# The loads of x for layer norm 1 are begun by GpSimd in place of ScalarE

## The chip, the cores and the metric

The kernel runs on one core of a Trainium2 chip. Its time is the device time of one execution in microseconds; the figure compared is the median of several runs. One execution was also taken by the hardware profiler, and all rows shown come from that one.

## The reference, cut to what matters

The input x has 4 images of 16 x 16 positions with 1024 channels, that is 1024 tokens. Layer 0 is a lambda layer between a group norm and a residual sum; layer 1 is causal attention over the 256 tokens of an image, and then a mixture of 8 experts.

```python
# layer 0
x = x + _L0_conv_ref(_gn(x), Wq, Wk, Wv, ..., rel_pos_emb)
#   inside: Lc = softmax(k) v^T;  Yc = q Lc           (content)
#           Lp = rel_pos_emb gathered, times v;  Yp = q Lp   (position)
#           Y = Yc + Yp
# layer 1
t = _to_tokens(x)
t = t + _L1_attn_ref(_ln_t(t), W_attn, b_attn, W_proj, b_proj)
t = t + _L1_ffn_ref(_ln_t(t), gate_w, gate_b, expert_w, expert_b)
x = _from_tokens(t, x)
```

All of it is float32. The place of this change is the residual sum of layer 0, x + Y, and the first layer norm of layer 1 behind it.

## The kernel before

The 1024 tokens are 8 tiles of 128 tokens; tile t = 2 * b + nt is half nt of image b. Channels are 8 blocks of 128. Large products are done by Strassen's scheme with 7 products of half blocks in place of 8.

Layer 0 starts from the transposed input in the buffer `xn` (8 blocks of 128 channels by 1024 tokens, 4 MB), which group norm overwrites. Products of it give q (line 311 and 392), the keys (line 423) and the values `v_T` (`v_product`, line 530, in seven products whose last is number 4). VectorE puts the products together (lines 535 to 554), and ScalarE scales the four quarters of `v_T` (line 557, four instructions).

The position part is built as products of windows of the embedding with q (line 502; the windows are copied by GpSimd, some by VectorE, line 499) into `two_T`, and from there 88 transfers of SP move rows of it into their places in the buffer `s0` (`move`, line 479, 16 to 64 KB each, one after the other in SP's queue). The moves that stand last are for the lower half of the positions (ni < 8), which only the last four tiles read.

Then line 572 begins the eight loads of the untransposed x, 512 KB each, into `x_at`. This buffer has the same home as `xn` (pool `x_pool`, one buffer), so it is free when the last v product has read `xn`. The loads go in the order in which the tiles are worked: nt = 1 of the four images, then nt = 0.

For each tile, `spread` (line 583) adds the content part to `s0` (products `pc`, line 444, added by VectorE at line 452), one tile ahead, multiplies `s0` by `v_T` (products `py`, line 595), and VectorE adds the result to x in `x_at` (line 602). `layer_norm` (line 184) follows on VectorE (statistics at line 189) and ScalarE (line 162). For six of the eight tiles the normalised rows are then turned into columns by way of DRAM: SP copies them out (line 204) and reads them back in quarters (line 174, four transfers a tile), and VectorE transposes those (line 179, two tiles later). GpSimd meanwhile adds the projection bias to x and writes it to `x_rows` in DRAM (lines 629 and 630). The buffers of the quarters are the spent buffers `emb` and `s_w`. Afterwards come the value products of the attention (line 656) with the weights `w_v`, loaded at line 121 by SP.

Each engine runs its instructions in the order of its queue. From line 613 on the order is the order of the program (`manual_schedule`); before that a scheduler of the framework orders the instructions of each engine, and the eight loads and the four scalings of v_T belong to this part. A transfer reports by a semaphore. The framework deals out eight of them in turn to the transfers that SP and ScalarE begin, in the order of the program, and eight others to those of GpSimd; before a transfer is begun, the former transfer on its semaphore must have landed. In the program before, ScalarE's queue holds three scalings of v_T, the first load of x, the fourth scaling, and the other seven loads. The first load waits for the end of the last v product and for the move that used its semaphore before it (the eighth from the last). The load of w_v (line 121) follows the last move in SP's queue, and the first copy of line 204 has the same semaphore as this load.

Of the kernel before, what the change touches and what calls it, by code (L numbers as in the profile page):

```python
# [39 lines left out]
P = 128  # L40
# [29 lines left out]
def kernel(  # L70
# [27 lines left out]
    nc = tc.nc  # L98
# [120 lines left out]
    with ExitStack() as layer0:  # L219
# [347 lines left out]
        xs = [x_at[:, t, :] for t in range(NT)]  # L567
        late = pool(x_home, "late", 2, side="right")
        tiles = [(b, nt) for nt in (1, 0) for b in range(B)]
        for b, nt in tiles:  # L570
            t = 2 * b + nt
            nc.scalar.dma_start(xs[t], x[ts(t, P), :])

# [7 lines left out]
        def spread(i):  # L583
            b, nt = tiles[i]
            t = 2 * b + nt
            if i == 0:
                content(b, nt)
            if i + 1 < NT:
                content(*tiles[i + 1])
            for hp in range(2):  # L590
                py = mm(f"py{t}_{hp}")
                for hl in range(2):
                    bh = b * HEADS0 + 2 * hp + hl
                    for mh in range(2):
                        nc.tensor.matmul(  # L595
                            py[:, ts(hl, M)],
                            s0[:, mh, ts(nt, S2), :, bh].rearrange("p i j -> p (i j)"),
                            v_T[:, mh, ts(b, M)],
                            start=(mh == 0),
                            stop=(mh == 1),  # L600
                        )
                nc.vector.tensor_add(xs[t][:, ts(hp, HALF)], xs[t][:, ts(hp, HALF)], py)
            return t
# [11 lines left out]
        for i in range(NT - 1):  # L615
            t = spread(i)
# [16 lines left out]
        t = spread(NT - 1)  # L633
# [4 lines left out]
    with ExitStack() as attention:  # L638
# [299 lines left out]
        with tc.manual_schedule():  # L938
            for i in range(written, len(steps) + lag):
                if i == written:  # L940
                    w_p.append(w_tile("w_p0", W_projT[:, :HALF]))
                if i == 28:
# [3 lines left out]
                    xs = [x_pool.tile([P, C], F32, tag=f"x{t}", name=f"xb{t}") for t in range(NT)]  # L946
# [5 lines left out]
                if 32 <= i < 34:  # L952
                    b, nt = tiles[NT - 34 + i]
                    t = 2 * b + nt
# [718 lines left out]
```

## Time and profile before

| | us |
|---|---|
| median of 3 runs | 1247.86 (1246.52 to 1249.15) |
| the profiled execution | 1245.87 |
| its span, first to last instruction | 1244.1 |
| TensorE busy | 1222.2 |
| VectorE busy | 741.6 |
| GpSimd busy | 404.0 |
| ScalarE busy | 220.0 |

The rows read as follows. A row of the timeline has the start and the length in us, the engine, the line of the kernel, the operation, the written and the read buffer, and the number of instructions; in brackets stands how long the engine was idle before it and what ended that. PE is TensorE, DVE VectorE, ACT ScalarE, POOL GpSimd, SP SyncE; ACTq and SPq are the queues in which ScalarE and SyncE begin transfers. A transfer's time to landing runs from its issue to the report that its data has arrived. The granted clock of TensorE is given as a share of its full speed.

### The profile page before, as it was taken

The numbers are of one execution on the slowest core, as the hardware profiler recorded it, in microseconds if no ns is written. First come the engines' busy times: TensorE is split into PE (matmuls) and PEld (weight loads), VectorE is DVE, ScalarE is ACT, GpSimd is POOL, SyncE is SP. The second block draws the span as 40 slices with busy tenths as digits, with TensorE's granted clock in tenths as the row PEclk, the third lists the DMA queues.
The fourth block names the chain that finished last, engine by engine and source line by source line (L and its number), as shares of the span: only waits on it lengthen the run. The fifth ranks groups of instructions, "written<-read, shape, count | busy, mean of one in ns | idle before, by whom it ended". The sixth has DMA issues, their size and how long they took to land.

```text
span 1244.1 us, 13324 instructions
## 1 busy us (share of the span) xinstructions
PE 1222.2 (98%) x4796; PEld 633.7 (51%) x4796; DVE 741.6 (60%) x1333; ACT 220.0 (18%) x514; POOL 404.0 (32%) x462
## 2 busy tenths in 40 slices
PE   9999998899999999999999999999999999999998
PEld 5445883678884444444444444444344434434443
DVE  5796635477432666657554867765656656565642
ACT  3310110221000222222121422110210111111110
POOL 0041340246000222222232115445452745363521
PEclk9999999899999999999999999999999999999999
DMA  9002023872202535353383657383856575656442
GB/s 349 21 1 81 5 53 72 303 251 69 68 1 68 153 106 156 105 174 108 101 286 118 196 218 254 72 236 89 240 129 173 109 229 154 156 128 190 101 82 54
DMA packets 94121, 169.77 MB, mean 136 GB/s; under 512 B 11968, under 2 KB 48848, under 8 KB 94048
## 3 DMA queue, kind: packets, MB, share of 16 engines
q1 hardware_dynamic: 75680, 112.68, 27.8%
q0 software_dynamic: 14992, 47.25, 16.2%
q10 hardware_dynamic: 3376, 8.91, 2.0%
q8 instruction: 40, 0.66, 0.2%
q14 instruction: 33, 0.27, 0.1%
HBM read 116.12 MB, written 48.50 MB: 132 GB/s over the span
## 4 chain that ended last, share of the span: by engine, by line
PE 89%; SPq 4%; DVE 3%; DMA 2%; ACT 1%; issue 1%; POOL 0%; DVEq 0%; ACTq 0%; POOLq 0%
PE p L1440 31%; PE pqk L656 16%; PE pv L656 8%; PE po L897 7%; SPq L479 4%; PE pq_pair L392 4%; PE left L1482 3%; PE pq L311 3%; PE pk L423 2%; PE sc L812 2%; PE pa L881 2%; PE rest L1496 2%; PE pT L502 1%; DMA w_v<-in_W_attnT_dram 1%; PE py L595 1%; PE last_pe L1598 1%
## 5 line engine op out<-in xcount | busy, mean ns | idle before, releaser
L1009 POOL DMA_INDIRECT w_e_xg<-rows,gather x146 | 157.0, 1075 | 57.3 <-issue 41.1
L1440 PE MATMUL p<-w_e,A 128*128 128x512 f32 x368 | 163.2, 593 | 1.3 <-DVE slot L1275 1.3
L854 POOL TENSOR_TENSOR s_q<-s_q,total 128x128 f32<-128x128 f32 (+1 forms) x128 | 66.1, 547 | 276.3 <-DVE total L851 276.3
L897 PE MATMUL po<-w_p,y_T 128*128 128x512 f32 x256 | 118.5, 604 | 0.0
L1440 PEld LDWEIGHTS p<-w_e,A 128*128 128x128 f32 x368 | 69.6, 190 | 89.9 <-issue 89.4
L1032 POOL DMA_INDIRECT out_dram<-y,add x32 | 56.5, 1767 | 178.2 <-ACT y L1446 114.8
L1440 PE MATMUL p<-T,S 128*128 128x512 f32 x256 | 112.7, 592 | 0.0
L1446 ACT ACTIVATE y<-y,slot 128x512 f32<-128x512 f32 x64 | 46.1, 721 | 335.5 <-DVE y L1454 177.4
L840 ACT ACTIVATE s_q<-s,top 128x256 f32<-128x256 f32 (+1 forms) x128 | 56.6, 443 | 186.2 <-issue 142.1
L656 PE MATMUL pqk<-ln,w_qk 128*128 128x512 f32 x192 | 85.6, 595 | 0.0
L1440 PEld LDWEIGHTS p<-T,S 128*128 128x128 f32 x256 | 48.6, 190 | 60.8 <-issue 60.5
L897 PEld LDWEIGHTS po<-w_p,y_T 128*128 128x128 f32 x256 | 45.9, 190 | 47.9 <-issue 46.9
L179 DVE STREAM_TRANSPOSE A<-w_e_xg 128x1024 f32<-128x1024 f32 x32 | 39.6, 1238 | 48.8 <-DMA w_e_xg<-rows,gather 48.7
L656 PE MATMUL pqk<-T,S_qk 128*128 128x512 f32 x128 | 58.5, 599 | 0.0
L656 PEld LDWEIGHTS pqk<-ln,w_qk 128*128 128x128 f32 x192 | 36.0, 190 | 43.4 <-issue 42.1
L1440 PE MATMUL p<-T,A 128*128 128x512 f32 x128 | 57.5, 592 | 0.0
L1440 PE MATMUL p<-w_e,S 128*128 128x512 f32 x128 | 57.5, 592 | 0.0
L311 PE MATMUL pq<-w_q,xn 128*128 128x512 f32 x96 | 44.5, 599 | 0.3 <-ACT xn L291 0.3
L656 PE MATMUL pv<-w_v,ln 128*128 128x256 f32 x192 | 43.5, 380 | 0.2 <-ACT ln L215 0.2
L1482 PE MATMUL left<-w_e,one 128*32 128x512 f32 x312 | 41.8, 593 | 0.0
L1440 PEld LDWEIGHTS p<-w_e,S 128*128 128x128 f32 x128 | 24.3, 190 | 30.6 <-issue 30.6
L1440 PEld LDWEIGHTS p<-T,A 128*128 128x128 f32 x128 | 24.3, 190 | 30.6 <-issue 30.1
(326 smaller groups left out, 1893.8 us busy)
## 6 DMA issues: line engine op xcount, KB each, us to landing
w_e<-in_expert_w_dram SPq DMA_DIRECT2D x14, 2048.0 KB, 12.2
s_rows<-s_q SPq DMA_DIRECT2D x32, 384.0 KB, 2.5
s_rows<-s_rows SPq DMA_DIRECT2D x128, 96.0 KB, 2.3
w_qk<-in_W_attnT_dram SPq DMA_DIRECT2D x8, 1024.0 KB, 5.9
xn<-in_xT_dram SPq DMA_DIRECT2D x8, 512.0 KB, 7.2
w_q<-in_Wq_dram SPq DMA_DIRECT2D x16, 256.0 KB, 7.0
x_at<-in_x_dram ACTq DMA_DIRECT2D x8, 512.0 KB, 8.9
w_v<-in_W_attnT_dram SPq DMA_DIRECT2D x2, 2048.0 KB, 11.3
```

What stands on the lines that cost most here:

```text
L311: nc.tensor.matmul(pq, xn[:, c, ts(t, P)], w_q[kc][:, c, :], start=(c == 0), stop=(c == NC - 1))
L392: nc.tensor.matmul(bank, a[:, c, :], b[:, c, :], start=(c == 0), stop=(c == NC // 2 - 1))
L479: nc.sync.dma_start(*m[2:])
L656: nc.tensor.matmul(bank, stationary(c), moving(c), start=(c == 0), stop=(c == NC // 2 - 1))
L840: nc.scalar.activation(blocks(h, qt), s[:, h, cols].rearrange("p (b f i) -> p b f i", f=Q, i=32), AF.Exp, bias=top[:, qt, h : h + 1], accu ...
L854: nc.gpsimd.tensor_mul(blocks(h, qt), blocks(h, qt), total[:, qt, h : h + 1].unsqueeze(2).unsqueeze(3).to_broadcast([P, 1 + qt, Q, 32]),)
L897: nc.tensor.matmul(po, y_T[:, c, ts(t, P)], w_p[j][:, c, :], start=(c == 0), stop=(c == NC - 1))
L1009: nc.gpsimd.indirect_dma_start(out=row[:, g, :], out_offset=None, in_=table[: (TOK - P) * Q, :] if e in SHORT else table, in_offset=bass.I ...
L1032: nc.gpsimd.indirect_dma_start(out=out[: TOK - P, :] if e in SHORT else out, out_offset=bass.IndirectOffsetOnAxis(ap=add[:slots, e, k : k ...
L1440: nc.tensor.matmul(bank, a[:, c, :], b[:, c, :], start=(c == 0), stop=(c == NC // 2 - 1))
L1446: nc.scalar.mul(y[i][:, ts(j, HALF)], y[i][:, ts(j, HALF)], slot[:, e, 1, 2 * pair + i : 2 * pair + i + 1])
L1482: nc.tensor.matmul(bank[ts(i, 32), :], stationary, w[of][j][:, c, :], start=(c == 0), stop=(c == NC - 1))
```

## The change

The loop at line 570 gives the eight loads to GpSimd's queue in place of ScalarE's. Nothing else in the program's text is changed.

```diff
         tiles = [(b, nt) for nt in (1, 0) for b in range(B)]
         for b, nt in tiles:
             t = 2 * b + nt
-            nc.scalar.dma_start(xs[t], x[ts(t, P), :])
+            nc.gpsimd.dma_start(xs[t], x[ts(t, P), :])
```

In the built program the four scalings of v_T then stand next to each other in ScalarE's queue. The eight loads stand in GpSimd's queue between its last window copy and its first addition of line 629. They take their semaphores from GpSimd's eight, so the later transfers of SP move on by eight turns, which is the same semaphore again for all but one: the load of w_v takes the semaphore that the first load of x had, and the first copy of line 204 now follows a move on its semaphore.

## The prediction

> **What bounds the kernel now.** I read three views of the page first: the busy times, the slices and the chain that ended last.
>
> ```profile
> PE 1222.2 (98%) x4796; PEld 633.7 (51%) x4796; DVE 741.6 (60%) x1333; ACT 220.0 (18%) x514; POOL 404.0 (32%) x462
> PE 89%; SPq 4%; DVE 3%; DMA 2%; ACT 1%; issue 1%; POOL 0%; DVEq 0%; ACTq 0%; POOLq 0%
> PE p L1440 31%; PE pqk L656 16%; PE pv L656 8%; PE po L897 7%; SPq L479 4%; PE pq_pair L392 4%; PE left L1482 3%; PE pq L311 3%; PE pk L423 2%; PE sc L812 2%; PE pa L881 2%; PE rest L1496 2%; PE pT L502 1%; DMA w_v<-in_W_attnT_dram 1%; PE py L595 1%; PE last_pe L1598 1%
> ```
>
> TensorE is the bound almost everywhere: it idles 22 us of 1244.1, so a change to some loads can only win where one of those few stalls lies. The pieces of the chain that are not TensorE (SP's queue at line 479, then the load of w_v) lie between 164 and 247 us, which is where the eight loads are begun (219.3 to 226.9 us). So I next read the timeline of TensorE there (start, duration, idle time before and what ended it):
>
> ```profile
> 206.43 7.03 PE L444 MATMUL pc<-q,k_q 128*128 128x512 f32 x16
> 213.30 0.59 PE L595 MATMUL py<-v_T,s 128*128 128x256 f32 x2
> 220.62 5.88 PE L595 MATMUL py<-v_T,s 128*128 128x256 f32 x14 [6.73 <-ACT v_T L557]
> 226.34 3.60 PE L444 MATMUL pc<-q,k_q 128*128 128x512 f32 x8
> 229.77 3.71 PE L595 MATMUL py<-v_T,s 128*128 128x256 f32 x16
> 249.11 3.70 PE L444 MATMUL pc<-q,k_q 128*128 128x512 f32 x8 [1.68 <-DVE s L452]
> ```
>
> Two stalls: 6.73 us that a ScalarE instruction ends, and 1.68 us that VectorE ends. After the first, 14 products take 5.88 us where 16 take 3.71 a round later. The timeline of ScalarE says what held it:
>
> ```profile
> 205.12 0.81 ACT L557 ACTIVATE v_T<-v_T,vp 128x512 f32<-128x512 f32 x1 [0.38 <-DVE v_T L552]
> 219.32 0.39 ACTq L572 DMA_DIRECT2D x_at<-in_x_dram  x1
> 219.76 0.81 ACT L557 ACTIVATE v_T<-v_T,vp 128x512 f32<-128x512 f32 x1 [13.83 <-DMA s<-two_T]
> 220.51 6.85 ACTq L572 DMA_DIRECT2D x_at<-in_x_dram  x7
> ```
>
> The fourth scaling of v_T stands in ScalarE's queue behind the first load of x, and that load waits until a move s<-two_T of SP has landed. Its own input was ready at 207.3 (line 554 on VectorE, 206.63 + 0.69). The order of the built program names the wait: SP's and ScalarE's DMAs take turns on eight completion semaphores, and the load must wait for the move that used its semaphore last, which SP issues at 217.2. Its real condition, the end of the last v product that reads the buffer, is met at 206.5. The other stall, by the timelines of SP and VectorE:
>
> ```profile
> 212.74 9.54 SPq L479 DMA_DIRECT2D s<-two_T  x15
> 222.38 0.53 SPq L121 DMA_DIRECT2D w_v<-in_W_attnT_dram  x1
> 237.06 0.35 SPq L204 DMA_DIRECT2D ln_rows<-ln_rows  x1
> 242.56 1.83 SPq L174 DMA_DIRECT2D emb<-ln_rows  x4
> ```
>
> ```profile
> 223.67 0.69 DVE L602 TENSOR_TENSOR x_at<-x_at,py 128x512 f32<-128x512 f32 x1 [9.48 <-DMA x_at<-in_x_dram]
> 247.24 1.25 DVE L179 STREAM_TRANSPOSE ln<-emb 128x1024 f32<-128x1024 f32 x1 [3.78 <-DMA emb<-ln_rows]
> ```
>
> The first layer-norm rows are ready at 230.76 (line 162), but their copy to DRAM starts at 237.06, because in the built program it has the same semaphore as w_v, which lands 14.61 us after its issue: it shares the DMA engines with the loads of x.
>
> **The change part by part.** *Removed from ScalarE:* one wait and eight issues (0.39 us median). The four scalings then follow each other, so the fourth runs at 207.4 to 208.2, and TensorE goes on at 213.30 without a gap. The 16 products of the first py take 3.55 us in later rounds (229.77 to 233.32) against 13.04 us now (213.30 to 226.34): 9.49 us less. Of this 6.73 is the idle time; 2.76 is the slower clock after it, 0.50 in the rows between 222.4 and 225 us. The table load of 1.28 us at 227.39 moves ahead too and is on no path (VectorE releases the next ScalarE step, 0.21 us).
>
> *Added to GpSimd:* eight issues, in its queue behind the window copies, which end at 183.8, and before line 629, first at 230.84. GpSimd is idle 47.01 us between. The order of the changed program gives these loads other completion semaphores, whose former users landed before 130 us, so they wait only for VectorE at 199.9, TensorE at 206.5 and an old ScalarE step. They start at about 206.6. The nearest row is line 951 (the same 512 KB from DRAM, on GpSimd): 0.55 us each and 5.0 to 9.1 us to land, so issues end at about 211.5. The first x is wanted at 215.3 (line 602 starts 1.97 us after py does, 229.77 to 231.74): 206.6 + 6.9, the median, gives 213.5; with 9.1 it is 215.7, 0.4 late, and a spare PSUM bank covers that. Later ones are wanted 7 us apart and land about 2.3 us apart. Cost: nothing, in the cover of the 16 pc products; without the cover each microsecond of a late first x is a microsecond of TensorE.
>
> The Trainium skill, "SBUF — State Buffer", section "SBUF: two separate sides", speaks against this: descriptors of GpSimd's DMAs cannot be written while VectorE runs in its two-port mode. VectorE is busy 3.44 of the 8.40 us from 206.6, with additions that read PSUM; even if each of these five blocked GpSimd for its whole 0.69 us, x would come 3.4 us later. No row here shows such a block. "DMA: Bandwidth & Descriptors", section "Issuing engines are not separate DMA queues", says another engine saves only issue time: by that alone the gain would be 8 x 0.39 = 3.1 us of ScalarE, none of it TensorE's. The 13.83 us row says that what is saved is a place in a queue.
>
> *Moved: the transfers.* The 4.19 MB of x now run beside 24 moves of SP, from 206.6 to 222.4, not beside w_v. A move lands in 2.0 us alone and 4.1 to 5.1 us beside the loads (those issued from 218.5 on). SP issues one each 0.637 us and reuses a semaphore each eighth, so 5.1 us is just what it bears without slowing. Then w_v starts at 222.4 as now.
>
> *The next thing that is late* is the first quarter chain, no longer held by w_v's semaphore (the copy of rows now follows an early move), but queued behind w_v on SP and in the transfers. With DMA engines full from 206.6 on, at the 398 GB/s of 225 to 237 us, in us of full engines: x 10.5; moves 5.6 (share 0.28 for 8.4 us, 0.44 for 7.4 us); w_v 5.3; the copied rows 1.3; the first write of x_rows 1.3. Sum 24.0; with 1.9 latency (fastest 512 KB write of GpSimd, 3.2, less 1.3) the copy lands at 232.5. (The same sum on the run of before puts w_v at 238.4; it landed at 237.0.) From landing to the transpose it took 4.75 us (242.49 to 247.24), so the transpose starts at 237.25 and the fifth round's pc 1.87 later, at 239.1 (before: 249.11). TensorE alone would be there at 213.30 + 3.55 + (249.11 - 1.68 - 226.34) = 237.94. So a stall of about 1.2 us stays.
>
> *Sum:* 249.11 - 239.1 = 10.0 us; or 9.49 + 1.68 - 1.2. Everything after is TensorE back to back, with waits relative to it, so the gain reaches the end. Bounds: w_v at the 7.9 us of the second w_v gives a transpose by about 235 and no stall, gain 11.2; w_v at 14.6 as now gives 237.0, copied rows 1.3, then 4.75 + 1.87: pc at 244.9, gain 4.2. I take the middle sum, since a bounded amount of data has to pass. The profiled execution took 1245.87 us (span 1244.1 and 1.8 around it) and would take 1235.9; the median of the runs is 1247.86, 2.0 above it, so 1237.9.
>
> **The rivals.** *The quarter chain takes the whole place of the stall.* If moves land in 7.2 us (the quarters s_rows beside GpSimd's loads at 618 to 630 us, median), SP issues one each 0.90 us, w_v starts 6.3 us later, and up to that much of the gain goes: gain 3 to 6, 1242 to 1245 us. For it: 5.1 is the edge already. Against: while moves wait, x finishes earlier, and the 7.2 us rows also queue behind a 2 MB load of SP.
>
> *Slower.* The same place, with a price: each us by which the moves end later than about 223 costs one. All the gain is gone when the transpose stands at 247.24 again, that is 10.0 us later, or 8 x (0.637 + 10.0/24) = 8.4 us to land; slower by over 2.5 us needs 9.3 us for all 24 moves. At 10 us it is 24 x 0.613 = 14.7 later and 4.7 slower: 1253. No 64 KB move in this trace comes near.
>
> *Nothing changes.* x is late after all: if the first load waits for GpSimd's descriptors or lands only at 223.7 as now, the py round drains as before and only the semaphore of w_v is gained, 0 to 1.7 us: 1246 to 1248. It would need 17 us to land, against 9.1 at most.
>
> **How the numbers follow.** Forecast (gain 6.5 to 11.2): 0.76. Chain takes most (gain 2.5 to 6.5): 0.13. Gain over 11.2, if the chain is faster and SP's later turns too: 0.03. No change: 0.04. Slower: 0.04. About 0.2%, 2.5 us, is what a measurement of this kernel can tell from no change. So faster 0.92, same 0.04, slower 0.04. The range reaches from 1247.86 - 11.2 less 0.4 for the spread of the runs, 1236.2, into the chain case at a gain of 5.4: 1242.5.
>
> **What would show it.** Right: the four scalings of v_T in a row by 208.5; TensorE without a gap at 213.3 and a granted clock of 1.0 through 225; x begun on GpSimd from 206.6, first landing before 215; w_v issued near 222.4 and landing before 233; line 204 issued within 1 us of w_v; the first transpose near 237; span near 1234. Wrong: a wait of VectorE at line 602 for x; SP's moves more than 0.7 us apart and w_v after 225; a gap of TensorE over 3 us before the fifth pc, all the more if its clock falls there again; or a new gap after 273 us that takes the gain back.

## The result, and the profile after

| | before | after |
|---|---|---|
| median, 20 runs each | 1246.47 us (1244.71 to 1249.15) | 1245.87 us (1245.33 to 1248.53) |
| span of the profiled execution | 1244.1 | 1244.2 |

The ratio after to before is 0.9997, with a 95% interval of 0.999 to 1.0003. The change moves nothing that can be measured; 1237.9 was predicted.

The timeline of TensorE in the stage of the change shows that the expected thing did happen, and what took it back.

```profile
205.95 7.03 PE L444 MATMUL pc<-q,k_q 128*128 128x512 f32 x16
212.82 3.69 PE L595 MATMUL py<-v_T,s 128*128 128x256 f32 x16
...
233.75 3.68 PE L595 MATMUL py<-v_T,s 128*128 128x256 f32 x16
245.93 6.48 PE L444 MATMUL pc<-q,k_q 128*128 128x512 f32 x8 [8.51 <-DVE s L452]
252.25 3.71 PE L595 MATMUL py<-v_T,s 128*128 128x256 f32 x16
```

Between 205.95 and 237.4 there is no gap: the stall of 6.73 us and the slow products behind it are gone, and the fourth py ends 10.0 us sooner than before (it began at 243.75 then, at 233.75 now; 0.48 of this was there at the start of the rows, since this execution came to the stage at 205.95 and that of before at 206.43). Then TensorE waits 8.51 us in one place and runs eight products in 6.48 us that took 3.70 before. The fifth py begins at 252.25; before it began at 252.65. Of 10.0 us, 0.4 are left, which is no more than the head start. (The rows count each product of the program twice, and for pc and py the text counts as they do. The first row of pc holds two tiles; the fifth pc is the fifth row.)

What was late there, by the timelines of GpSimd (POOL), SP and VectorE (DVE):

```profile
206.67 4.21 POOL L572 DMA_DIRECT2D x_at<-in_x_dram  x8 [23.31 <-PE pv L530]
226.40 0.53 SPq L121 DMA_DIRECT2D w_v<-in_W_attnT_dram  x1
227.03 0.52 SPq L204 DMA_DIRECT2D ln_rows<-ln_rows  x1
238.45 2.33 SPq L174 DMA_DIRECT2D emb<-ln_rows  x4
214.77 0.69 DVE L602 TENSOR_TENSOR x_at<-x_at,py 128x512 f32<-128x512 f32 x1 [1.06 <-PE py L595]
244.06 1.25 DVE L179 STREAM_TRANSPOSE ln<-emb 128x1024 f32<-128x1024 f32 x1 [10.60 <-DMA ln_rows<-ln_rows]
```

VectorE no longer waits for x (1.06 us for TensorE at line 602). But SP's moves end 4.0 us later, so w_v is begun at 226.40 and not at 222.38; the first tile's copy of line 204 stands right behind it and takes until 238.4 to land; the quarters are read only then, and the transpose, which the fifth pc waits for, comes at 244.06 (247.24 before, 237.25 predicted).

The transfers between 206.6 and 238.4 us (40 slices of 0.795 us each; busy tenths, then the rate):

```profile
DMA  4929999999999999999998398255999999999700
GB/s 101 120 77 397 407 372 379 377 316 310 362 348 366 362 332 349 322 331 374 307 226 173 140 407 199 65 39 162 404 410 425 381 301 286 381 410 428 304 36 10
```

In the first three slices, though the loads were begun at 206.67, only 77 to 120 GB/s flow; from the fourth to the twentieth (209.0 to 222.5) over 300, at a mean of 354. Then SP is still busy with its last moves, and eight slices (222.5 to 228.9) run at a mean of 176 GB/s, until w_v's bytes flow at over 400. The windows give the same, and TensorE's clock with it (stretch, us, busy PE, PEld, DVE, ACT, POOL, granted clock, DMA share, GB/s):

```profile
215.00:222.40 7.40, 7.40 (x27) 5.56 (x27) 4.87 (x11) 1.44 (x2) 1.54 (x1) 1.00 1.04 346
222.40:225.00 2.60, 2.60 (x9) 1.68 (x9) 1.50 (x4) 0.00 (x0) 1.38 (x2) 1.00 0.81 196
225.00:237.00 12.00, 12.00 (x44) 9.25 (x43) 5.56 (x15) 2.89 (x4) 5.09 (x3) 1.00 0.86 302
237.00:250.00 13.00, 4.49 (x7) 1.98 (x7) 5.55 (x12) 0.20 (x1) 0.73 (x2) 0.67 0.65 203
```

The moves in flight beside the loads took 6.1 to 7.0 us to land, where they took 2.0 before; those issued from 209.1 to 216.7 this long:

```profile
DMA to landing us min/median/max: 6.1/6.4/6.7
```

The ones issued just before them took 6.9 us, and the last ones beside the loads, issued up to 219.3, took 7.0.

### The profile page after: what moved, and what is told of

Same layout as the page of the kernel before. It is cut to its first block, busy times and chain, and to the rows that moved or that the text cites. A ratio compares the mean times of both kernels' runs of the same rounds, so it can differ in the third digit from the quotient of the medians.

```text
span 1244.2 us, 13333 instructions
## 1 busy us (share of the span) xinstructions
PE 1221.8 (98%) x4796; PEld 632.7 (51%) x4796; DVE 740.5 (60%) x1333; ACT 219.9 (18%) x514; POOL 409.1 (33%) x470
## 4 chain that ended last, share of the span: by engine, by line
PE 73%; issue 13%; POOL 5%; DVE 3%; DMA 3%; SPq 2%; ACT 1%; POOLq 0%; DVEq 0%; ACTq 0%
PE p L1440 31%; PE pv L656 8%; PE po L897 6%; POOL s_q L854 5%; PE pq_pair L392 4%; PE left L1482 3%; PE pq L311 3%; PE pqk L656 3%; PE pk L423 2%; PE rest L1496 2%; PE pv L530 2%; PE pT L502 2%; SPq L479 1%; DMA s<-two_T 1%; DMA ln_rows<-ln_rows 1%
## 5 line engine op out<-in xcount | busy, mean ns | idle before, releaser
L179 DVE STREAM_TRANSPOSE A<-w_e_xg 128x1024 f32<-128x1024 f32 x32 | 39.6, 1238 | 49.6 <-DMA w_e_xg<-rows,gather 47.6
```

The costliest lines, as they stand in the source:

```text
L179: nc.vector.transpose(row_T[:, :, :slots].rearrange("p c (g j) -> p g c j", j=32), row[:, : slots // 32, :].rearrange("p g (c i) -> p g c ...
```

## The experiments

The theory after the result: the early loads do take away both early stalls, and the stage is then set by the chain of the first tile (copy of line 204, quarters of line 174, transpose of line 179), which is late because the loads slow SP's moves and because w_v's 2 MB stand ahead of it; the low clock behind the gap is a third term. The rivals were that the place in SP's queue alone counts, and that the bytes count whatever the order. e4, e7 and e8 start from the kernel before, all others from the changed one; each is compared with the kernel before on the same chip. Where an edit adds lines, the lines of the kernel behind it have moved on by as many. The profiled executions come to this stage at different times (the first pc begins between 205.67 and 207.13 us), so a difference of about 1 us between the rows of two runs says little. `TB` below stands for `W_attnT[:, 2 * C : 2 * C + HALF]`.

### Is it w_v ahead of the copy? (e1, e5, e7)

e1 begins w_v by ScalarE behind the second tile's layer norm, at 227.77, so that the copy is ahead of it in time and in another queue:

```diff
-        w_v = [w_tile("w_v0", TB)]
...
             layer_norm(...)
+            if i == 1:
+                w_v = [w_tile("w_v0", TB, queue=nc.scalar)]
```

> The changed kernel, with the load of w_v begun by ScalarE behind the layer norm of the second tile (about 227.8 us) and not by SP between the last move and the first copy of rows (226.4 us). Theory A (the copy is late because 2 MB stand ahead of it in SP's own queue): the copy is issued near 226.4 and lands by 232, not 238.4; the first transpose stands at 235 to 237.5, not 244.06; the gap of TensorE before the fifth pc falls from 8.5 us to 0 to 2 us, its clock stays at 1.0, and the kernel is 6 to 10 us faster than before, 1236 to 1241. Rival B (the same number of bytes has to pass the DMA engines first, whichever queue begins them): w_v is begun at almost the same moment, so the copy still lands at 236 or later and the gain is at most 2 us.

Measured: 1243.83 us, ratio 0.9971 (0.996 to 0.9982). The copy landed in 5.4 us in place of 11.35, but now the quarters ran beside w_v and took 7.5 to 7.8 us. The timelines of TensorE and SP:

```profile
244.01 6.74 PE L444 MATMUL pc<-q,k_q 128*128 128x512 f32 x8 [5.40 <-DVE s L452]
227.68 0.53 SPq L204 DMA_DIRECT2D ln_rows<-ln_rows  x1
233.14 1.96 SPq L174 DMA_DIRECT2D emb<-ln_rows  x4
```

The copy landed 5.3 us sooner and the transpose (242.14) only 1.9, in an execution that came to the stage 1.2 us later: the place in SP's queue is part of it, but w_v's bytes are in the way from another queue too. e5 puts w_v behind the fourth tile's layer norm (`if i == 3`, else as e1), behind the whole first chain:

> The changed kernel, with the load of w_v begun by ScalarE behind the layer norm of the fourth tile (about 242 us), so that neither its place in SP's queue nor its 2.1 MB stand ahead of the first copy and its quarters. Theory A (what bounds the changed kernel is w_v ahead of the first tile's copy and quarters): the copy goes out when the moves end (226.4 to 227.5), lands by 232, the quarters land in 3 to 4 us, the first transpose stands at 236 to 237.5 and the gap before the fifth pc is 0 to 2 us at a clock of 1.0: 9 to 11 us less than before, 1235 to 1238. Rival B (the slowed moves alone hold the chain): gap still above 4 us, gain at most 5 us. w_v itself is wanted at about 262 us, 20 us later; if it is late the first pv waits for it and the gain falls.

Measured: 1240.58 us, ratio 0.9948 (0.9935 to 0.9962). The copy landed in 5.3 us, the quarters in 3.1; the transpose stood at 237.43 and the gap shrank to 1.50 us with no loss of clock. In the profiled execution w_v then met the third tile's quarters, and a gap of 3.74 us came there, so the time missed the 1235 to 1238 us that were expected, though the first chain did what was expected of it:

```profile
239.30 3.70 PE L444 MATMUL pc<-q,k_q 128*128 128x512 f32 x8 [1.50 <-DVE s L452]
257.27 6.24 PE L444 MATMUL pc<-q,k_q 128*128 128x512 f32 x8 [3.74 <-DVE s L452]
```

Is the late w_v good by itself, without the change? e7 makes the same edit in the kernel before:

> The kernel before with the same late load of w_v as in the run that begins it behind the fourth tile's layer norm; x is still begun by ScalarE at 219.3 us. If the change of the loads is needed for the gain: the stall of 6.73 us and the slow py behind it stay, and only the 1.68 us gap can go: 1244 to 1247. If w_v was the whole matter: the same time as with the changed loads, 1235 to 1238.

Measured: 1245.7 us, ratio 0.9989 (0.998 to 0.9998). The early stall stays at 6.89 us. So late w_v alone gives about 1.4 us, and with the changed loads 6.5: the change is worth about 5 us once w_v is out of its way.

### Is the low clock a cost of its own? (e2, e11)

e2 puts 28 products of the identity, in a buffer that nothing reads, into the gap before the fifth pc:

```diff
+            if i == 3:
+                warm = ps.tile([P, 2, HALF], F32, tag="sc", name="warm", bufs=1)
+                for _ in range(28):
+                    nc.tensor.matmul(warm[:, 0, :P], ident, ident, start=True, stop=True)
             return t
```

> The changed kernel, with 28 products of the identity with itself (0.27 us each, some 7.6 us) put on TensorE between the py of the fourth tile and the pc of the fifth, where it idles 8.51 us; their result is read by nobody. If the fall of the granted clock behind the gap is a cost of its own: the eight products of the fifth pc take 3.4 us, not 6.48, and the kernel is 2.5 to 3 us faster than the changed one, about 1243. If the clock is not the reason for the 6.48 us, or what follows waits for something else in any case: no difference over 0.5 us.

Measured: 1245.09 us, ratio 0.9985 (0.9974 to 0.9997); the profiled span is 1241.5 against 1244.2. The windows show the clock at 1.00 from 237 to 250 us, and the timeline the fifth pc at its full speed:

```profile
237.95 6.41 PE L606 MATMUL warm<-ident 128*128 128x128 f32 x56
245.48 3.70 PE L444 MATMUL pc<-q,k_q 128*128 128x512 f32 x8 [1.11 <-DVE s L452]
```

(Each product is counted twice in these rows.) The pc is 2.8 us shorter and the span 2.7; the median moved only 0.8, and by the ratios 1.5. The eleven runs of e2 fall into two groups: five with a mean granted clock of 0.999 or 1.0 took 1242.74 to 1244.66 us, six with 0.997 or 0.998 took 1245.09 to 1246.10, about as long as the changed kernel. The profiled execution is one of the five. In the six the clock was lower somewhere in spite of the idle products; no trace shows where. The same test on a kernel with a shorter gap (e6 below, with 14 products):

> The kernel with w_v begun by GpSimd, and 14 products of the identity by itself, whose result nothing reads, in the gap before the fifth pc. Theory now (the clock after the gap costs about 3 us beside the gap itself): the fifth pc takes 3.7 us and not 6.5, and the time falls by 2.5 to 3 us against the run without them, to about 1237.8. Rival (the slow clock costs nothing since work behind it has slack): 1240.7, as without.

Measured: 1239.06 us, ratio 0.9933 (0.9918 to 0.9949), 1.6 us less than e6; the fifth pc took 3.70 us. The direction holds in both, and in e14 against e12 below. But no pair is clear of its intervals: by the ratios the idle products are worth 1.5, 1.9 and 0.4 us, each with an uncertainty of 1.5 us or more. That the low clock is a cost of its own is shown in the profiled executions (2.8 us of pc in e2, and in e11 against e6); how much of it is left in the median is not.

### Is it the moves, slowed by the loads of x? (e3, e13)

e3 loads four tiles of x at line 572 and the other four one by one behind the writes of line 630:

```diff
-        for b, nt in tiles:
+        for b, nt in tiles[:4]:
...
                 nc.gpsimd.dma_start(x_rows[ts(t, P), :], xs[t])
+                if i < 4:
+                    b, nt = tiles[4 + i]
+                    nc.gpsimd.dma_start(xs[2 * b + nt], x[ts(2 * b + nt, P), :])
```

> The changed kernel, with only four loads of x begun at 206.7 us; the other four follow one by one behind the write of x_rows of each of the first four tiles (from about 224 us). Theory A (moves of SP slow down for as long as loads of x are in flight, 24 moves then end at 226.3 and not at 222.4): loads are in flight for half the time, so the last move goes out near 224 and w_v with it; copy, transpose and the fifth pc come 2 us earlier than in the changed kernel, and the gap falls to some 6 us: 1242 to 1244. Rival (moves are slowed by something else, such as GpSimd's way of beginning transfers): w_v still goes out at 226 and the time is that of the changed kernel, 1246.

Measured: 1248.05 us, ratio 1.0011 (1.0001 to 1.0021). w_v and the copy were begun 2.1 us sooner, as expected, and it brought nothing, since the copy took 12.9 us to land:

```profile
224.30 0.53 SPq L121 DMA_DIRECT2D w_v<-in_W_attnT_dram  x1
224.93 0.83 SPq L204 DMA_DIRECT2D ln_rows<-ln_rows  x1
237.89 2.00 SPq L174 DMA_DIRECT2D emb<-ln_rows  x4
```

The moves were faster because less was in flight; what was not moved then (the windows from 215 to 222.4 show 105 GB/s against 346) had to be moved later, beside the copy. This run could not tell the moves from the rest, so e13 repeats it with the late w_v of e5:

> Against the run with late w_v (1240.6 us, SP's moves end at 227.2, transpose at 237.4): the second half of x is put off too. Theory (the moves, slowed by the loads of x, hold the chain back by themselves once w_v is away): moves end at 224.2 as in the run with half of x, copy lands near 230, transpose at 234.5 to 235.5, the gap of 1.50 us before the fifth pc goes, and the time is 1 to 1.5 us less than 1240.6 unless a later tile's chain takes it. Rival (it is the bytes, whoever they belong to): the late half of x and the write of x_rows hold the copy, the transpose stays at 237 or later, 1240.5 to 1243 us.

Measured: 1244.63 us, ratio 0.9976 (0.9964 to 0.9988). The median move landed in 2.6 us and SP was through with them at 224.0, yet the copy took 6.4 us, the quarters 6.8 us, and the transpose stood at 238.71, later than in e5:

```profile
224.11 0.53 SPq L204 DMA_DIRECT2D ln_rows<-ln_rows  x1
230.54 2.15 SPq L174 DMA_DIRECT2D emb<-ln_rows  x4
```

So the theory that the slowed moves hold the chain by themselves fell: the bytes that are put off come back in the chain's way.

### Is it the loads or the order on ScalarE? (e4, e8)

The kernel before, with the four scalings of v_T written in order ahead of ScalarE's eight loads:

```diff
+        with tc.manual_schedule():
+            for j in range(2):
+                for th in range(2):
+                    nc.scalar.activation(
...
+            for b, nt in tiles:
+                t = 2 * b + nt
+                nc.scalar.dma_start(xs[t], x[ts(t, P), :])
```

> The kernel before, loads of x still begun by ScalarE, but all four scalings of v_T put ahead of them in its queue. This takes away the wait that I read as the cause of the 6.73 us stall and nothing else, though the semaphores move on by one turn, so that the copy of rows no longer shares w_v's. If that wait was worth its length: TensorE does the first py at 213.3 and the kernel gains 5 to 9 us. If it only hid the chain behind it (x from 219.3 us, then w_v, then copy, quarters, transpose): TensorE stalls elsewhere, at line 602 for x and before the fifth pc, the transpose stands at 243 to 247 us, and the time is within 3 us of before.

Measured: 1254.66 us, ratio 1.006 (1.0044 to 1.0077), slower. The first py came without a gap at 212.76, but the turns of the semaphores had shifted, and the eighth load of x waited for w_v's, with all of ScalarE behind it:

```profile
220.06 18.85 ACTq L573 DMA_DIRECT2D x_at<-in_x_dram  x8
238.94 1.28 ACT L134 ACT_TABLE_LOAD   x1 [30.60 <-DMA w_v<-in_W_attnT_dram]
```

That wait spoils the comparison, so e8 adds the late w_v of e5 to it:

> The kernel before with the late load of w_v, and with all four scalings of v_T ahead of the loads of x in ScalarE's queue; the loads still begin at 219.3 us. It parts the two things that the change gives: the scaling 12 us sooner, and x 12 us sooner. If the scaling is what counts: py at 213 without a gap, and nearly the time of the changed loads with late w_v, 1235 to 1239. If x is wanted as well: py of the first tile at 213, then TensorE waits 4 to 5 us for line 602 and x (223.7), its clock falls for a while, and 4 to 7 us of the gain are missing: 1240 to 1244.

Measured: 1244.83 us, ratio 0.9984 (0.9973 to 0.9996). TensorE passes the first py and then waits for x at the second:

```profile
223.92 5.54 PE L596 MATMUL py<-v_T,s 128*128 128x256 f32 x16 [3.83 <-DVE x_at L603]
```

With the same late w_v, early x (e5) is 4.25 us faster. Freeing the scalings alone only moves the stall to VectorE's wait for x.

### Can the hole in the transfers be filled? (e6, e9, e10, e12, e14)

Other orders of the same transfers. e6 begins w_v by GpSimd right behind x (`queue=nc.gpsimd` at line 613), at 211.1. e9 leaves w_v to SP and begins the first tile's copy by GpSimd:

```diff
-        nc.sync.dma_start(rows.rearrange("n f c -> n (f c)"), ln)
+        (nc.gpsimd if t == 1 else nc.sync).dma_start(rows.rearrange("n f c -> n (f c)"), ln)
```

e10 is e9 with w_v by ScalarE as in e1 (at 227.75, behind the second tile's layer norm and not the first, as its expectation says), e12 is e6 and e9 together, and e14 is e12 with the 14 identity products of e11.

> The changed kernel, with w_v begun by GpSimd straight behind the eight loads of x (about 213 us). The same bytes stand ahead of the first copy as in the changed kernel, but the engines are kept full, as my sum took it. Theory A by bytes (my sum): x and w_v have passed by about 227 to 229 us, moves end at 228 to 230 as they are slowed for longer, the copy lands at 232 to 233.5, the transpose stands at 237 to 239, and the gain is 7 to 10 us: 1236 to 1239. Rival (moves are slowed without bound by GpSimd's loads in flight): moves end after 232, the transpose is at 242 or later, and the gain is under 4 us.

> The changed kernel, but the first tile's copy of line 204 is begun by GpSimd, right behind the loads of x and not behind SP's moves and w_v. Theory now (the chain copy, quarters, transpose of the first tile sets the time, and the copy is late because it stands behind 2 MB of w_v): copy begun at about 221, landed by 226 to 228, the quarters begun behind w_v at about 227.5 and landing in 7 to 8 us beside its bytes, as in the run with w_v by ScalarE, so the transpose at about 236 to 237 and the fifth pc near 238.5 to 239: 1237 to 1240 us, ratio 0.994. Rival (only w_v's bytes being out of the way counts, wherever the copy stands): quarters land at 240 or later, 1244 us or more.

> As the last, and w_v is begun by ScalarE behind the first layer norm (about 228) and not by SP. Theory now: the quarters are begun at about 226.5 to 227.5, ahead of w_v, land in 3 us, the transpose stands in time near 232 to 234 and the gap before the fifth pc is gone; the second tile's quarters may meet w_v's bytes. 1235.5 to 1238 us, ratio 0.991 to 0.993. Rival (some other wait stands right behind the chain and takes the place): no better than 1240.5.

> The changed kernel with w_v and the first tile's copy both begun by GpSimd, w_v first. Theory now: the copy is begun at about 221 and lands by 229 to 231 beside w_v and the last moves, the quarters follow in 3 us, the transpose at 234 to 236, no gap before the fifth pc or one under 1.5 us and no slow clock: 1236 to 1238.5 us. Rival (the copy lands behind w_v whatever queue it is in): transpose at 239 as with w_v alone, 1240.7.

> w_v and the first copy begun by GpSimd, with 14 identity products in the gap, whose result nothing reads. If the gap and the slow clock are separate terms, the fifth pc takes 3.7 us in place of 5.4 and the time is 1.5 to 2 us less than the 1239.2 without the products: 1237.2 to 1237.7. Rival (the products only fill a gap that is set by the transpose and what follows is held by a later transfer): 1239.

| run | copy begun, landed | quarters land in | transpose | gap, fifth pc | median | ratio (95%) |
|---|---|---|---|---|---|---|
| after | 227.03, 238.4 | 3.5 to 3.7 | 244.06 | 8.51, 6.48 | 1245.87 | 0.9997 (0.999 to 1.0003) |
| e6 | 229.08, 234.7 | 2.6 to 2.9 | 239.31 | 3.73, 6.53 | 1240.66 | 0.9948 (0.9934 to 0.9962) |
| e9 | 220.97, by 227.5 | 9.1 to 10.1 | 239.52 | 4.05, 5.34 | 1240.80 | 0.9945 (0.993 to 0.9961) |
| e10 | 220.94, by 227.6 | 8.0 to 8.5 | 239.47 | 4.03, 6.61 | 1241.36 | 0.9946 (0.9931 to 0.9961) |
| e12 | 221.74, 234.4 | 2.9 to 3.2 | 239.05 | 2.83, 5.40 | 1239.19 | 0.9928 (0.9914 to 0.9942) |
| e14 | 221.47, 234.2 | 2.9 to 3.2 | 238.86 | filled, 3.64 | 1237.81 | 0.9925 (0.991 to 0.994) |

e6 is the plainest of them, since one argument is changed and the order of w_v, copy and quarters is that of the changed kernel (w_v is begun at 211.06 and not at 226.40):

```profile
229.08 0.36 SPq L204 DMA_DIRECT2D ln_rows<-ln_rows  x1
234.69 1.86 SPq L174 DMA_DIRECT2D emb<-ln_rows  x4
239.31 1.25 DVE L179 STREAM_TRANSPOSE ln<-emb 128x1024 f32<-128x1024 f32 x1 [5.83 <-DMA emb<-ln_rows]
```

The copy is begun 2.1 us later than in the changed kernel and lands 3.7 us sooner, the transpose comes 4.75 us sooner, and the median is 5.2 us less. Whichever piece is put first, the transpose comes between 238.86 and 239.71 (e11 has the last); counted from the first load of x it is 31.7 and 31.8 us in e12 and e14 and 32.6 to 33.0 in the others. The transposes expected at 232 to 237 for e9, e10 and e12 all missed, and so did the times of e6 and of these three, each because the piece put off was late in turn: the quarters beside w_v in e9 and e10, the copy beside w_v in e12 (12.7 us to land). In e12 the transfers between 206.6 and 238.4 us have no hole before the copy lands:

```profile
DMA  3365999999999999999999999999999999923889
GB/s 94 71 52 197 426 381 366 356 321 329 352 339 375 348 321 313 354 322 343 350 347 344 319 370 314 381 309 325 357 300 384 412 407 403 407 83 102 286 200 299
```

So about 239 is where these orders end; that no order of the same bytes ends sooner is not shown. The changed kernel's 244.06 is 5 us above it, because it let the engines run half empty and then put the copy and the quarters one after the other behind w_v. The best of these kernels, e14, is 0.75% faster than the kernel before; e12, without the idle products, 0.72%. In e14 TensorE meets no gap from the first pc to the value products of the attention:

```profile
234.15 3.68 PE L595 MATMUL py<-v_T,s 128*128 128x256 f32 x16
237.67 3.29 PE L606 MATMUL warm<-ident 128*128 128x128 f32 x28
240.79 3.64 PE L444 MATMUL pc<-q,k_q 128*128 128x512 f32 x8
244.27 3.70 PE L595 MATMUL py<-v_T,s 128*128 128x256 f32 x16
```

## Why the prediction was wrong, by its own steps

*Removed from ScalarE: right.* The last scaling ran at 206.88 and TensorE went on at 212.82 without a gap, at a clock of 1.00. The 9.49 us were gained, and with the head start of 0.48 us TensorE stood 10.0 us ahead of the kernel before at the fourth py.

*Added to GpSimd: right.* The eight issues began at 206.67 (206.6 predicted) and took 0.53 us each; x was in time. Of the block of GpSimd's descriptors that "SBUF — State Buffer", section "SBUF: two separate sides", of the Trainium skill speaks of, this trace shows no sign: VectorE was busy 3.23 of the 8.40 us from 206.6, and the issues ran back to back. Whether any of those instructions was in the two-port mode no row says, so this is no test of it.

*Moved, the transfers: wrong in size.* "5.1 us is just what it bears without slowing. Then w_v starts at 222.4 as now." The moves took 6.1 to 7.0 us, SP fell behind, and w_v was begun at 226.40, 4.0 us later. The prediction named this sign itself (w_v after 225), and its first rival rests on it, with 7.2 us and 6.3 us of delay.

*The quarter chain: the step that failed.* "With DMA engines full from 206.6 on, at the 398 GB/s" put the landing of the copy at 232.5. Its first two terms, x and moves (10.5 and 5.6), were to fill the engines to 222.7, and the high rate does end at 222.5; that is partly luck, since SP still had moves to begin until 226.3. The sum added bytes as if one pool fed the engines, but w_v can't flow before SP has begun it, behind the slowed moves. So the landing was 5.9 us later, at 238.4. e6 and e12, whose engines stay full from the start of the loads' flow to the copy's landing, put it at 234.7 and 234.4: 3.7 to 4.0 of the 5.9 are the hole, and w_v was begun 4.0 us later. The other 1.9 to 2.2 remain there too. "Full from 206.6 on" was not met either: the first three slices carry 99 GB/s on average, which against the 354 of the next seventeen is an estimated 1.7 us. No run parts this from the rest. From landing to transpose it took 5.7 us and not 4.75, another 0.9.

*The sum: a term left out.* The starting point was high too: 1247.86 was the median of three runs, and that of twenty is 1246.47, 1.4 us less. The pc behind the gap took 6.48 us and not 3.70: 2.8 us. The prediction had shown this very cost behind the first stall (2.76 us) and looked for it as a sign of a wrong result, but no bound of the chain had it, since each priced the wait alone. Predicted gain 10.0, less 5.9, 0.9 and 2.8, is 0.4, which is what the fifth py shows.

*The rivals.* "The quarter chain takes the whole place of the stall" named the right place; its 3 to 6 us of gain fit the 3.2 us by which the fifth pc began sooner, but it had no term for the clock either. "Slower" let the whole gain go only with the transpose at 247.24 again; it went with the transpose at 244.06, by the same missing term. "Nothing changes" came nearest with its 1246 to 1248, for a wrong reason, since x was not late.

"DMA: Bandwidth & Descriptors", section "Issuing engines are not separate DMA queues", of the Trainium skill says that transfers interleave on the same 16 engines whoever begins them, and that another engine saves issue time only. For the bytes the runs agree (e6, e9, e10, e11, e12 and e14 have the transpose within 0.9 us). For the queue they don't: a place behind another transfer's wait cost ScalarE 13.83 us, and a place behind SP's moves cost w_v its hole.

Left open: e5 and e13 have profiled executions of the same length (1243.43 and 1243.42 us) and medians 4.05 us apart; the profile of e5 is the longest of its five runs, and no trace shows what the shorter ones did at the third tile (their mean granted clock was 0.997 or 0.998 against 0.996, which suggests a shorter gap or none). An order that loads w_v still later than that tile was not tried.

## What to carry to other kernels

When a stall goes, the next chain has to be summed by queues and not by bytes alone: ask for each large transfer which instruction begins it, and what the newly early transfers do to those that stand ahead of it. Price a new gap of TensorE with the products behind it at the lower clock, not only with the wait. And where a change frees an engine but moves nothing in the end, look for the two or three transfers that now stand in the wrong order: here moving two of them made a change of 0.0% into one of 0.7%.

## What the runs showed of the hardware beside that

The price of a gap in clock is not in step with its length. Eight products of pc that take 3.6 to 3.7 us took, behind a gap of 2.83 us, 5.40 (e12); behind 3.73, 6.53 (e6); behind 4.05, 5.34 (e9); behind 5.40, 6.74 (e1); behind 10.74, 5.08 (e3). Behind 0.91, 1.50 and 1.68 us they took 3.70 (e11, e5 and the kernel before), and once, in e13, behind 3.68 too:

```profile
260.19 3.70 PE L444 MATMUL pc<-q,k_q 128*128 128x512 f32 x8 [3.68 <-DVE s L452]
```

Idle products of 128 columns, which nothing reads, were enough to keep the clock at 1.00 from 237 to 250 us in the profiled executions of e2, e11 and e14.

Small transfers pay for large ones on another queue in latency: a 64 KB move took 2.0 us in the kernel before, ahead of the loads, and 6.1 to 7.0 beside GpSimd's loads of 512 KB, and a quarter of 128 KB took 2.6 to 2.9 us with little else in flight (e6) and 7.5 to 10.1 beside w_v's 2 MB (e1, e9 and e10).
